# Layer 0's first product in a four-layer graph network: seven block products for eight from the fifth unit on, and group weights in two rotating buffers

## The chip, the cores and the metric

The kernel runs on one core of a Trainium2 chip. Its time is the device time of one execution in microseconds (us). Before the change the median of three runs is 2221.21 us (2220.69 to 2221.58). One more execution was profiled; it took 2220.84 us, and its span, from the first to the last instruction in the trace, is 2218.8 us.

The engines are named as in the profile: PE is TensorE (matmul), PEld its weight load, DVE is VectorE, ACT is ScalarE, POOL is GpSimd, and SP is SyncE, which here only issues DMAs. [...]

## The reference

The input is 128 graphs of 64 nodes with 256 features in float32, with one 64x64 adjacency matrix per graph. Four layers follow each other, each as `x = layernorm(x + layer(x, adj))`. The change touches layer 0. It works on five groups of nodes (25, 9, 7, 6 and 6 nodes out of the first 25), each with two graph convolutions of its own weights:

```python
A = adj + eye; dinv = deg ** -0.5; norm_adj = dinv * A * dinv
support = einsum('bnd,de->bne', x, W)          # W1: 256 x 512, then W2: 512 x 256
out = relu(einsum('bnm,bme->bne', norm_adj, support) + b)
...
h     = graph_conv(x[:, idx], adj[:, idx][:, :, idx], W1[g], b1[g])
out_g = graph_conv(h,         adj[:, idx][:, :, idx], W2[g], b2[g])
fused[:, idx] += softmax(fusion_w)[g] * out_g
```

Layers 1 and 2 are graph convolutions over all 64 nodes. Layer 3 is a gated recurrent cell, run five times per graph; it takes most of the time.

## The kernel before

Layer 0 packs graphs block-diagonally. A tile holds as many graphs as fit into 126 rows, and a unit is four tiles, up to 504 columns (UNITS, L61). The groups come in the order 1, 2, 3, 4, 0. This gives 16 units: units 0 to 2 belong to group 1 (504, 504 and 144 columns), 3 and 4 to group 2 (448 each), 5 and 6 to group 3 (504 and 264), 7 and 8 to group 4 (504 and 264), 9 to 15 to group 0 (six of 500, then 200). "The fifth unit" is unit 4.

A unit passes through these steps, each a function:

- `load0` (L342): DMAs of the adjacency blocks (`a`, L357) and of x (`xg`, L359). For groups 3 and 4 a row range is two runs of three nodes, so that a tile takes four DMAs.
- `prep` (L364): DVE adds the identity, sums the degrees (`ae`, L374), POOL raises to the power -0.5, DVE builds the block-diagonal matrix A, PE transposes it (L393), and DVE evicts and scales it to `AT` (L397).
- `aggregate` (L399): PE multiplies x by AT (`pa`, L407), ACT copies the result to `ag` (L412).
- `hidden` (L415): the first product, W1 (256 x 512) by `ag`. There are four blocks of 128 output rows by two blocks of 128 input rows: eight block products of all columns (`ph`, L422), each pair closed by a relu on ACT into `hg` (L425).
- `support` (L428): `hg` by W2, tile by tile, in two halves of two tiles (`ps`, L436).
- `add` (L449): PE multiplies by AT once more (`po`, L458), ACT scales and applies relu, DVE adds into F.
- `finish` (L484), for group 0 only: transposes back, adds the residual, layer norm, stores.

A loop (L565) runs a software pipeline over these units. Iteration i issues the loads of unit i+3, `add` of i-1, `aggregate` of i+1, `support` of i, `finish` of i-1, `prep` of i+2 and `hidden` of i+1. PE runs in exactly the order in which this is written (the manual schedule, L329). The other engines' order is made by a scheduler from priorities, from `high_priority` blocks and from `issue_after`, which pins an instruction behind another. In the same iterations `others` (L514) normalises the 39 nodes that layer 0 leaves as they are (`xo`, loaded at L511, stored at L520), and the steps of layers 1 and 2 for the first two chunks of graphs (`mid`, L219) begin.

All group weights are resident: W1 for five groups and W2 for five groups, one DMA of 512 KB each (L534, L537). Those of groups 1 and 2 are issued ahead of the loop's iteration 0, that of W1 for group 3 in iteration -1, and the other five in iteration 0.

Layer 3 computes its gates with seven block products for eight already (class `Gates`, L695): a 2x2-block product in the Strassen-Winograd form. `factors` (L660) makes the three combined weight blocks, `sums` (L687) the combined inputs on POOL, and the seven products go into three PSUM banks, a, b and d, with copies on ACT (L727) and adds on DVE (L729, L733, L739).

Of the kernel before, what the change touches and what calls it, by code (L numbers as in the profile page):

```python
# [16 lines left out]
NG, NJ = 5, 25  # L17
# [50 lines left out]
def gnn_stack(  # L68
# [118 lines left out]

    def load_adj(c):
        a64 = keep.tile([128, NP, N], F32, name="a64", bufs=2)
        nc.sync.dma_start(a64, av[c])  # L190
        adjs[c] = a64
# [140 lines left out]
    with ExitStack() as c0:  # L332
        w0 = c0.enter_context(tc.tile_pool(name="w0", bufs=1))
        work = c0.enter_context(tc.tile_pool(name="work0", bufs=1))
        W1 = w0.tile([128, NG, 2, HID], F32, name="W1")
        W2 = w0.tile([128, NG, 4, D], F32, name="W2")
# [3 lines left out]
        loads, A, AG, HG, S2, Z, XO = {}, {}, {}, {}, {}, {}, {}  # L340

# [73 lines left out]
        def hidden(i):  # L415
            u = UNITS[i]
            ag0 = AG.pop(i)
            hg = keep.tile([128, 4, 512], F32, tag="NI", name="hg", bufs=2)
            for e in range(4):
                p = psum0("ph")[:, : u.cols]  # L420
                for k in range(2):
                    nc.tensor.matmul(  # L422
                        p, W1[:, u.g, k, e * 128 : (e + 1) * 128], ag0[:, k, : u.cols], start=k == 0, stop=k == 1
                    )
                nc.scalar.activation(hg[:, e, : u.cols], p, AF.Relu, bias=b1[:, u.g * 4 + e : u.g * 4 + e + 1])  # L425
            HG[i] = hg

        def support(i):  # L428
            u = UNITS[i]
            hg, s2 = HG.pop(i), []  # L430
            for v in range(0, len(u.tiles), 2):
                p = psum0("ps").rearrange("p (t d) -> p t d", t=2)
                ts = range(v, min(v + 2, len(u.tiles)))
                for t in ts:
                    for e in range(4):
                        nc.tensor.matmul(  # L436
                            p[: u.rows[t], t - v, :], hg[:, e, u.off[t] : u.off[t] + u.rows[t]], W2[:, u.g, e, :],
                            start=e == 0, stop=e == 3,
                        )
# [93 lines left out]
        def load_first(g):  # L533
            nc.sync.dma_start(W1[:, g], w1[g].rearrange("(k p) e -> p k e", p=128))  # L534

        def load_second(g):
            nc.sync.dma_start(W2[:, g], w2[g].rearrange("(k p) e -> p k e", p=128))  # L537
# [26 lines left out]
        g0 = next(i for i, u in enumerate(UNITS) if u.g == 0)  # L564
        for i in range(-2, NU + 1):  # L565
            if i >= 0:
                stage(load0, i + 3)
            stage(add, i - 1)
            if i:
                stage(aggregate, i + 1)  # L570
            early_stage(i, 0)
            stage(support, i)
            if not i:
                aggregate(1)
            if i == NU:
# [3 lines left out]
            if i == -1:  # L579

                hidden(0)
                with tc.issue_after(evictions[0].ins):
                    prep(1)
            else:
                stage(prep, i + 2)
                stage(hidden, i + 1)
# [5 lines left out]
            elif i == -1:  # L592
                load_second(2)
                load_first(3)
            elif i == 0:
                load_second(3)
                for g in (4, 0):
                    load_first(g)
                    load_second(g)
# [60 lines left out]
    def factors(w, w21):  # L660

        nc.vector.tensor_add(w[:, 4, :], w21, w[:, 3, :])
        nc.gpsimd.tensor_sub(w[:, 6, :], w[:, 0, :], w21)
        nc.vector.tensor_sub(w[:, 5, :], w[:, 4, :], w[:, 0, :])
        nc.vector.tensor_sub(w[:, 2, :], w[:, 1, :], w[:, 5, :])
# [21 lines left out]
    def sums(a, name):  # L687

        t = work.tile([128, 4, H], F32, tag="T" + name, name="T" + name, bufs=2)
        nc.gpsimd.tensor_sub(t[:, 0:2, :], a[:, :, H:], a[:, 0, :].rearrange("p (s n) -> p s n", s=2))  # L690
        nc.gpsimd.tensor_sub(t[:, 2, :], a[:, 1, H:], t[:, 0, :])
        nc.gpsimd.tensor_sub(t[:, 3, :], a[:, 1, :H], t[:, 2, :])
        return t

    class Gates:  # L695

        def __init__(self, C, sides, name):
            self.C, self.sides, self.name = C, sides, name  # L700
            self.copies = {}

        def multiply(self, bank, i):
            for g, side in enumerate(self.sides):
                for m, (w, q, a, t) in enumerate(side):
                    rhs = {
                        1: a[:, 0, :H], 2: a[:, 1, :H], 3: a[:, 1, H:], 4: t[:, 3, :], 5: t[:, 0, :], 6: t[:, 2, :],
                        7: t[:, 1, :],
                    }[i]
                    nc.tensor.matmul(  # L710
                        bank[:, g, :], w[:, q, i - 1, :], rhs, start=i in (1, 2, 5) and g == 0 and m == 0,
                        stop=m == len(side) - 1, skip_group_check=True,
                    )

        def bank(self, s):
            return pg.tile([128, 2, H], F32, tag="pg", name=f"p{s}{self.name}")

        def product(self, i):
            C = self.C
            if i == 1:  # L720
                self.a = self.bank("a")
            if i in (1, 6, 7, 4):
                self.multiply(self.a, i)
                if i != 4:
                    c = self.copies[i] = work.tile([128, 2, H], F32, tag="copy", name=f"c{i}", bufs=4)
                    with tc.high_priority():
                        nc.scalar.copy(c, self.a)  # L727
                if i == 7:
# [245 lines left out]
```

## Time and profile before

| | before |
|---|---|
| runs, median (lowest to highest) | 2221.21 us (2220.69 to 2221.58) |
| span of the profiled execution | 2218.8 us |
| mean granted PE clock | 0.993 |
| PE busy | 2180.1 us, 98% |
| DVE / ACT / POOL busy | 1376.3 / 1004.5 / 582.5 us |
| layer 0's stretch | from 0 to about 308 us |
| `hidden`, a unit of 500 columns | 6.71 us on the chain |

The page gives busy time by engine, then 40 slices of the span with one digit each (tenths busy), and the clock that PE was granted. A group of instructions has its line of the kernel, its engine, what it writes and reads, its count, busy time and mean duration. In a timeline, a bracket at the end of a line gives the idle time of the engine ahead of it and what released it. A windows row gives, for a stretch of the span, the busy time of PE, PEld, DVE, ACT and POOL (with instruction counts), the clock, the share of the DMA engines and their GB/s.

### The profile page before, as it was taken

The numbers are of one execution on the slowest core, as the hardware profiler recorded it, in microseconds if no ns is written. First come the engines' busy times: TensorE is split into PE (matmuls) and PEld (weight loads), VectorE is DVE, ScalarE is ACT, GpSimd is POOL, SyncE is SP. The second block draws the span as 40 slices with busy tenths as digits, with TensorE's granted clock in tenths as the row PEclk, the third lists the DMA queues.
The fourth block names the chain that finished last, engine by engine and source line by source line (L and its number), as shares of the span: only waits on it lengthen the run. The fifth ranks groups of instructions, "written<-read, shape, count | busy, mean of one in ns | idle before, by whom it ended". The sixth has DMA issues, their size and how long they took to land.

```text
span 2218.8 us, 30141 instructions
## 1 busy us (share of the span) xinstructions
PE 2180.1 (98%) x11526; PEld 1912.2 (86%) x11526; DVE 1376.3 (62%) x3068; ACT 1004.5 (45%) x1850; POOL 582.5 (26%) x639
## 2 busy tenths in 40 slices
PE   7999999999999999999999999999999999999997
PEld 5677888888888889888889898888898898888886
DVE  4443667666766666666756676657666666556546
ACT  2333334445544454445454454455454544455443
POOL 3210123222222223223222222222222222222222
PEclk9999999999999999999999999999999999999998
DMA  6540210000100000000100010001000000000000
GB/s 188 169 128 22 57 46 3 1 3 1 40 2 3 1 20 22 4 1 8 34 1 3 1 41 1 4 1 41 1 1 1 20 10 1 1 10 10 1 1 20
DMA packets 54172, 51.12 MB, mean 23 GB/s; under 512 B 20878, under 2 KB 49036, under 8 KB 54028
## 3 DMA queue, kind: packets, MB, share of 16 engines
q1 hardware_dynamic: 49524, 43.90, 6.5%
q0 software_dynamic: 1936, 4.83, 0.7%
q8 instruction: 91, 1.49, 0.3%
q10 hardware_dynamic: 2568, 0.47, 0.1%
q14 instruction: 53, 0.43, 0.1%
HBM read 32.40 MB, written 16.78 MB: 22 GB/s over the span
## 4 chain that ended last, share of the span: by engine, by line
PE 91%; DMA 3%; DVE 2%; issue 1%; SPq 1%; POOL 1%; ACT 0%; POOLq 0%; ACTq 0%; DVEq 0%
PE parz L710 25%; PE pdrz L710 12%; PE pan L710 12%; PE pa L209 9%; PE pbrz L710 6%; PE pdn L710 6%; PE pT L751 4%; PE pbn L710 3%; PE ph L422 3%; PE ps L436 3%; PE pd L285 2%; PE pd L306 2%; DMA xo<-in_x_dram 1%; PE pa L407 1%; PE po L458 1%
## 5 line engine op out<-in xcount | busy, mean ns | idle before, releaser
L727 ACT COPY c<-parz 128x512 f32<-128x512 f32 x240 | 140.9, 587 | 322.5 <-PE parz L710 322.0
L710 PE MATMUL parz<-Th,WHH 128*128 128x256 f32 x960 | 285.8, 379 | 0.0
L710 PE MATMUL parz<-Ta,V 128*128 128x256 f32 x960 | 285.5, 379 | 0.0
L690 POOL TENSOR_TENSOR Th<-hn 128x512 f32<-128x512 f32 x64 | 81.6, 1274 | 774.0 <-DVE hn L811 588.5
L808 ACT ACTIVATE NI<-NI,bih 128x512 f32<-128x512 f32 x160 | 115.6, 722 | 206.2 <-DVE NI L804 206.1
L727 ACT COPY c<-pan 128x512 f32<-128x512 f32 x240 | 141.0, 587 | 149.6 <-PE pan L710 149.6
L710 PEld LDWEIGHTS parz<-Ta,V 128*128 128x128 f32 x960 | 182.4, 190 | 24.7
L710 PEld LDWEIGHTS parz<-Th,WHH 128*128 128x128 f32 x960 | 176.2, 190 | 20.9 <-ACT c L727 0.2
L781 ACT ACTIVATE RZ<-RZ,brz 128x512 f32<-128x512 f32 x160 | 116.1, 727 | 138.6 <-DVE RZ L739 138.6
L690 POOL TENSOR_TENSOR Ta<-agg 128x512 f32<-128x512 f32 x80 | 102.2, 1277 | 260.6 <-ACT agg L213 260.6
L739 DVE TENSOR_TENSOR RZ<-pdrz,c 128x512 f32<-128x512 f32 x80 | 55.1, 688 | 173.9 <-PE pdrz L710 173.9
L710 PE MATMUL pan<-Ta,V 128*128 128x256 f32 x480 | 143.2, 380 | 0.9 <-ACT c L727 0.9
L710 PE MATMUL pan<-Th,WHH 128*128 128x256 f32 x480 | 142.7, 379 | 0.0
L138 POOL TENSOR_TENSOR rs<-ve,mhalf 128x4 f32<-128x4 f32 (+2 forms) x66 | 68.7, 1042 | 252.3 <-DVE ve L136 226.4
L733 DVE TENSOR_TENSOR NI<-pbn,c 128x512 f32<-128x512 f32 x80 | 55.4, 692 | 127.6 <-PE pbn L710 108.6
L209 PEld LDWEIGHTS pa<-A,h 128*128 128x128 f32 x1024 | 124.4, 192 | 3.3
L729 DVE TENSOR_TENSOR NI<-pdn,c 128x512 f32<-128x512 f32 x80 | 55.2, 690 | 114.4 <-ACT c L727 114.4
L209 PE MATMUL pa<-A,h 128*128 128x128 f32 x1024 | 124.6, 275 | 0.0
L809 DVE TENSOR_TENSOR RZ<-hn,NI 128x512 f32<-128x512 f32 x128 | 87.9, 687 | 48.5 <-ACT NI L808 48.5
L811 DVE TENSOR_TENSOR hn<-RZ,NI 128x512 f32<-128x512 f32 x160 | 109.9, 687 | 1.8
L810 DVE TENSOR_TENSOR RZ<-RZ 128x512 f32<-128x512 f32 x160 | 109.7, 685 | 1.8
L436 PE MATMUL ps<-W,hg 128*125 128x256 f32 (+5 forms) x464 | 104.2, 382 | 0.0
(199 smaller groups left out, 5076.1 us busy)
## 6 DMA issues: line engine op xcount, KB each, us to landing
out_dram<-xt SPq DMA_DIRECT2D x32, 256.0 KB
W<-in_w_dram SPq DMA_DIRECT2D x10, 512.0 KB
xt<-xb SPq DMA_DIRECT2D x32, 156.0 KB
xo<-in_x_dram SPq DMA_DIRECT2D x9, 512.0 KB
xb<-xo SPq DMA_DIRECT2D x9, 512.0 KB
xt<-xa SPq DMA_DIRECT2D x32, 100.0 KB
xg<-in_x_dram SPq DMA_DIRECT2D x25, 125.0 KB
xa<-xg SPq DMA_DIRECT2D x25, 125.0 KB
```

The lines of the kernel that those rows point to most:

```text
L138: nc.gpsimd.tensor_tensor(rs[:r, :n], ve[:r, :n], mhalf[:r, :n], ALU.pow)
L209: nc.tensor.matmul(p[:, q * 128 : (q + 1) * 128], src[:, q, k * 128 : (k + 1) * 128], m[:, q, :], start=True, stop=True)
L436: nc.tensor.matmul(p[: u.rows[t], t - v, :], hg[:, e, u.off[t] : u.off[t] + u.rows[t]], W2[:, u.g, e, :], start=e == 0, stop=e == 3,)
L690: nc.gpsimd.tensor_sub(t[:, 0:2, :], a[:, :, H:], a[:, 0, :].rearrange("p (s n) -> p s n", s=2))
L710: nc.tensor.matmul(bank[:, g, :], w[:, q, i - 1, :], rhs, start=i in (1, 2, 5) and g == 0 and m == 0, stop=m == len(side) - 1, skip_group_ ...
L727: nc.scalar.copy(c, self.a)
L751: nc.tensor.transpose(p[:, q * 128 : (q + 1) * 128], src(q, k), ident)
L781: nc.scalar.activation(RZ[:, q, 0, :], RZ[:, q, 0, :], AF.Sigmoid, bias=b[0])
L808: nc.scalar.activation(n, n, AF.Tanh, bias=bih[:, 4 + j : 5 + j])
L809: nc.vector.tensor_sub(d, self.hT[:, j, :], n)
L810: nc.vector.tensor_mul(d, d, z)
L811: nc.vector.tensor_add(self.hn[:, j, :], d, n)
```

## The change

- `hidden` becomes a generator. For units 4 to 14 it forms the first product by seven block products of half the columns each, two output halves per product: 14 matmuls of half width for 8 of full width. Units 0 to 3 and unit 15 (200 columns, less than H = 256) keep eight.
- Its products are spread over PE's order: the generator is advanced twice ahead of the second half of `support` of the unit before (it sets up the sums, then runs product 1), three times after `prep` (products 6, 2, 5), once more at the end (7), once after the next `add` (4), and to its end after the next `aggregate` (3).
- `factors`, `sums` and `Gates` move up, so that both layers use them; for layer 0, three copies of bank a on ACT and three adds on DVE join the products, and eight relus of half width stand for four.
- The weights of a group live in two rotating buffers. W1 is loaded by four DMAs (three into a tile with room for seven blocks, one into a separate tile W21), W2 by one. Groups 3, 4 and 0 are loaded in iterations 2 and 3, 4 and 5, 6 and 7. The combined weight blocks are made in iterations 1, 3, 5 and 7, pinned behind the latest AT eviction and power.

```diff
+    def factors(w, w21):
+
+        nc.vector.tensor_add(w[..., 4, :], w21, w[..., 3, :])
+        nc.gpsimd.tensor_sub(w[..., 6, :], w[..., 0, :], w21)
+        nc.vector.tensor_sub(w[..., 5, :], w[..., 4, :], w[..., 0, :])
+        nc.vector.tensor_sub(w[..., 2, :], w[..., 1, :], w[..., 5, :])
+
...
+    def sums(a, pool, name, bufs=2):
+
+        h = a.shape[2] // 2
+        t = pool.tile([128, 4, H], F32, tag="T" + name, name="T" + name, bufs=bufs)[:, :, :h]
+        nc.gpsimd.tensor_sub(t[:, 0:2, :], a[:, :, h:], a[:, 0, :].rearrange("p (s n) -> p s n", s=2))
+        nc.gpsimd.tensor_sub(t[:, 2, :], a[:, 1, h:], t[:, 0, :])
+        nc.gpsimd.tensor_sub(t[:, 3, :], a[:, 1, :h], t[:, 2, :])
+        return t
...
+        def product(self, i):
+            C, h = self.C, self.h
+            if i == 1:
+                self.a = self.bank("a")
+            if i in (1, 6, 7, 4):
+                self.multiply(self.a, i)
+                if i != 4:
+                    c = self.pool.tile([128, 2, H], F32, tag="copy", name=f"c{i}", bufs=4)[:, :, :h]
+                    self.copies[i] = c
+                    with tc.high_priority():
+                        nc.scalar.copy(c, self.a)
+                if i == 7:
+                    nc.vector.tensor_add(C[:, :, 1, h:], self.d, self.copies.pop(7))
+            elif i == 2:
+                b = self.bank("b")
+                self.multiply(b, i)
+                nc.vector.tensor_add(C[:, :, 0, :h], b, self.copies.pop(1))
+            else:
+                if i == 5:
+                    self.d = self.bank("d")
+                self.multiply(self.d, i)
+                if i == 3:
+                    nc.vector.tensor_add(C[:, :, 0, h:], self.d, self.copies.pop(6))
...
-        W1 = w0.tile([128, NG, 2, HID], F32, name="W1")
-        W2 = w0.tile([128, NG, 4, D], F32, name="W2")
...
+        W1, W21, W2 = {}, {}, {}
...
-        def hidden(i):
+        def hidden(i, seven=True):
+
             u = UNITS[i]
-            ag0 = AG.pop(i)
+            w, w21 = W1[u.g], W21[u.g]
+            ag0 = AG.pop(i)[:, :, : u.cols]
             hg = keep.tile([128, 4, 512], F32, tag="NI", name="hg", bufs=2)
-            for e in range(4):
-                p = psum0("ph")[:, : u.cols]
-                for k in range(2):
-                    nc.tensor.matmul(
-                        p, W1[:, u.g, k, e * 128 : (e + 1) * 128], ag0[:, k, : u.cols], start=k == 0, stop=k == 1
-                    )
-                nc.scalar.activation(hg[:, e, : u.cols], p, AF.Relu, bias=b1[:, u.g * 4 + e : u.g * 4 + e + 1])
             HG[i] = hg
+            b = lambda e: b1[:, u.g * 4 + e : u.g * 4 + e + 1]
+            if not seven or u.cols < H:
+                for _ in range(5):
+                    yield
+                for e in range(4):
+                    p = psum0("ph")[:, : u.cols]
+                    for k in range(2):
+                        wk = w21[:, e // 2, :] if e % 2 > k else w[:, e // 2, 3 if e % 2 else k, :]
+                        nc.tensor.matmul(p, wk, ag0[:, k, :], start=k == 0, stop=k == 1)
+                    nc.scalar.activation(hg[:, e, : u.cols], p, AF.Relu, bias=b(e))
+                return
+            h = u.cols // 2
+            with tc.high_priority():
+                t = sums(ag0, work, "0", 1)
+            C = hg.rearrange("p (g j) n -> p g j n", g=2)[:, :, :, : u.cols]
+            g7 = Gates(C, [[(w, g, ag0, t)] for g in range(2)], work, lambda s: psum0("ph" + s))
+            for m in (1, 6, 2, 5, 7, 4, 3):
+                yield
+                g7.product(m)
+                for g in range(2):
+                    j, f = {2: (0, slice(0, h)), 7: (1, slice(h, 2 * h)), 3: (0, slice(h, 2 * h))}.get(m, (1, slice(0, h)))
+                    if m in (2, 7, 3, 4):
+                        nc.scalar.activation(C[:, g, j, f], C[:, g, j, f] if m != 4 else g7.a[:, g, :], AF.Relu, bias=b(2 * g + j))
 
         def support(i):
+
             u = UNITS[i]
             hg, s2 = HG.pop(i), []
             for v in range(0, len(u.tiles), 2):
+                yield v + 2 >= len(u.tiles)
                 p = psum0("ps").rearrange("p (t d) -> p t d", t=2)
                 ts = range(v, min(v + 2, len(u.tiles)))
                 for t in ts:
                     for e in range(4):
                         nc.tensor.matmul(
-                            p[: u.rows[t], t - v, :], hg[:, e, u.off[t] : u.off[t] + u.rows[t]], W2[:, u.g, e, :],
+                            p[: u.rows[t], t - v, :], hg[:, e, u.off[t] : u.off[t] + u.rows[t]], W2[u.g][:, e, :],
                             start=e == 0, stop=e == 3,
                         )
...
         def load_first(g):
-            nc.sync.dma_start(W1[:, g], w1[g].rearrange("(k p) e -> p k e", p=128))
+            W1[g] = w0.tile([128, 2, 7, 128], F32, tag="W1", name=f"W1{g}", bufs=2)
+            W21[g] = w0.tile([128, 2, 128], F32, tag="W21", name=f"W21{g}", bufs=2)
+            v = w1[g].rearrange("(k p) (q e) -> p k q e", p=128, q=2)
+            for k in range(2):
+                nc.sync.dma_start(W1[g][:, :, k, :], v[:, k, :, :128])
+            nc.sync.dma_start(W21[g], v[:, 0, :, 128:])
+            nc.sync.dma_start(W1[g][:, :, 3, :], v[:, 1, :, 128:])
 
         def load_second(g):
-            nc.sync.dma_start(W2[:, g], w2[g].rearrange("(k p) e -> p k e", p=128))
+            W2[g] = w0.tile([128, 4, D], F32, tag="W2", name=f"W2{g}", bufs=2)
+            nc.sync.dma_start(W2[g], w2[g].rearrange("(k p) e -> p k e", p=128))
...
+        cur = iter(())
         for i in range(-2, NU + 1):
             if i >= 0:
                 stage(load0, i + 3)
             stage(add, i - 1)
+            next(cur, None)
             if i:
                 stage(aggregate, i + 1)
+            for _ in cur:
+                pass
             early_stage(i, 0)
-            stage(support, i)
+
+            nxt = hidden(i + 1, i > 2) if 0 <= i + 1 < NU else iter(())
+            if 0 <= i < NU:
+                for last in support(i):
+                    if last and i:
+                        next(nxt, None)
+                        next(nxt, None)
+            else:
+                next(nxt, None)
+                next(nxt, None)
             if not i:
                 aggregate(1)
+                next(nxt)
+                next(nxt)
             if i == NU:
                 folds = [products(0, q) for q in range(3)]
             stage(finish, i - 1, g0)
             early_stage(i, 1)
             if i == -1:
 
-                hidden(0)
+                for _ in nxt:
+                    pass
                 with tc.issue_after(evictions[0].ins):
                     prep(1)
             else:
                 stage(prep, i + 2)
-                stage(hidden, i + 1)
+                for _ in range(3):
+                    next(nxt, None)
+            next(nxt, None)
+            cur = nxt
             if i == -2:
                 load0(1, powers[0])
                 load_second(1)
...
                 load_first(2)
             elif i == -1:
                 load_second(2)
-                load_first(3)
-            elif i == 0:
-                load_second(3)
-                for g in (4, 0):
-                    load_first(g)
-                    load_second(g)
+
+            elif i == 1:
+                with tc.issue_after(evictions[-1].ins), tc.issue_after(powers[-1].ins):
+                    factors(W1[2], W21[2])
+            elif i in (2, 4, 6):
+                g = {2: 3, 4: 4, 6: 0}[i]
+                load_first(g)
+            elif i in (3, 5, 7):
+                g = {3: 3, 5: 4, 7: 0}[i]
+                load_second(g)
+                with tc.issue_after(evictions[-1].ins), tc.issue_after(powers[-1].ins):
+                    factors(W1[g], W21[g])
...
-    def sums(a, name):
-
-        t = work.tile([128, 4, H], F32, tag="T" + name, name="T" + name, bufs=2)
-        nc.gpsimd.tensor_sub(t[:, 0:2, :], a[:, :, H:], a[:, 0, :].rearrange("p (s n) -> p s n", s=2))
-        nc.gpsimd.tensor_sub(t[:, 2, :], a[:, 1, H:], t[:, 0, :])
-        nc.gpsimd.tensor_sub(t[:, 3, :], a[:, 1, :H], t[:, 2, :])
-        return t
```

In layer 3 only the arguments change (`sums(..., work, ...)`, `Gates(..., work, lambda s: bank(...))`).

More of the change, by code (lines that the diff above doesn't have):

```diff
@@ new lines, in gnn_stack, with __init__, multiply, bank @@
+    class Gates:
+        def __init__(self, C, sides, pool, bank):
+            self.C, self.sides, self.pool, self.new_bank = C, sides, pool, bank
+            self.h = C.shape[3] // 2
+            self.copies = {}
+        def multiply(self, bank, i):
+            h = self.h
+            for g, side in enumerate(self.sides):
+                for m, (w, q, a, t) in enumerate(side):
+                    rhs = {
+                        1: a[:, 0, :h], 2: a[:, 1, :h], 3: a[:, 1, h:], 4: t[:, 3, :], 5: t[:, 0, :], 6: t[:, 2, :],
+                        7: t[:, 1, :],
+                    }[i]
+                    nc.tensor.matmul(
+                        bank[:, g, :], w[:, q, i - 1, :], rhs, start=i in (1, 2, 5) and g == 0 and m == 0,
+                        stop=m == len(side) - 1, skip_group_check=True,
+                    )
+        def bank(self, s):
+            return self.new_bank(s)[:, : 2 * self.h].rearrange("p (g n) -> p g n", g=2)
+        def product(self, i):
[21 more added lines that the diff above has]
+                    nc.vector.tensor_add(C[:, :, 0, h:], self.d, self.copies.pop(6))
@@ L658, in gnn_stack @@
     V = [work.tile([128, 3, 7, 128], F32, name=f"V{l}") for l in range(L)]
[L660 to L665, printed above, removed]
     def fold():
@@ L685, in fold, with bank @@
                 yield
-    def sums(a, name):
-        t = work.tile([128, 4, H], F32, tag="T" + name, name="T" + name, bufs=2)
-        nc.gpsimd.tensor_sub(t[:, 0:2, :], a[:, :, H:], a[:, 0, :].rearrange("p (s n) -> p s n", s=2))
-        nc.gpsimd.tensor_sub(t[:, 2, :], a[:, 1, H:], t[:, 0, :])
-        nc.gpsimd.tensor_sub(t[:, 3, :], a[:, 1, :H], t[:, 2, :])
-        return t
[L695 to L728, printed above, removed]
-                    nc.vector.tensor_add(C[:, :, 1, H:], self.d, self.copies.pop(7))
-            elif i == 2:
-                b = self.bank("b")
-                self.multiply(b, i)
-                nc.vector.tensor_add(C[:, :, 0, :H], b, self.copies.pop(1))
-            else:
-                if i == 5:
-                    self.d = self.bank("d")
-                self.multiply(self.d, i)
-                if i == 3:
-                    nc.vector.tensor_add(C[:, :, 0, H:], self.d, self.copies.pop(6))
+    def bank(s):
+        return pg.tile([128, 2 * H], F32, tag="pg", name="p" + s)
     class Chunk:
@@ L759, in state_of_layer2 @@
             if not k:
-                self.th = sums(self.hT, "h")
+                self.th = sums(self.hT, work, "h")
         def messages(self, h=None):
             self.agg = gather(self.xt if h is None else h, self.A01, "agg", work, "agg", 2)
-            self.ta = sums(self.agg, "a")
+            self.ta = sums(self.agg, work, "a")
         def rz(self, i):
@@ L769, in rz @@
                 self.g = Gates(
-                    self.RZ, [[(WHH, q, self.hT, self.th), (V[self.l], q, self.agg, self.ta)] for q in (0, 1)], "rz"
+                    self.RZ, [[(WHH, q, self.hT, self.th), (V[self.l], q, self.agg, self.ta)] for q in (0, 1)],
+                    work, lambda s: bank(s + "rz"),
                 )
@@ L786, in n @@
                 self.gn = Gates(
-                    self.NI, [[(V[self.l], 2, self.agg, self.ta)], [(WHH, 2, self.hT, self.th)]], "n"
+                    self.NI, [[(V[self.l], 2, self.agg, self.ta)], [(WHH, 2, self.hT, self.th)]],
+                    work, lambda s: bank(s + "n"),
                 )
@@ L826, in turn @@
                 if not k:
-                    self.th = sums(self.hT, "h")
+                    self.th = sums(self.hT, work, "h")
             else:
```

## The prediction

> **What bounds the kernel now.** I read the page first: the shares, the slices with the clock, the chain by engine.
>
> ```profile
> span 2218.8 us, 30141 instructions
> PE 2180.1 (98%) x11526; PEld 1912.2 (86%) x11526; DVE 1376.3 (62%) x3068; ACT 1004.5 (45%) x1850; POOL 582.5 (26%) x639
> PE   7999999999999999999999999999999999999997
> PEclk9999999999999999999999999999999999999998
> ```
>
> TensorE is busy 98% of the span at full clock. A micro-second of its work saved is a micro-second of time, unless a wait fills it. Layer 0 ends near 308 us, so I then read the chain of work up to 335 us, for what one matmul record costs (each F32 matmul leaves two records):
>
> ```profile
> 161.19 1.78 PE po L458 x16
> 157.62 3.56 PE ph L422 x16
> 181.08 6.91 PE ps L436 x32
> 188.42 6.71 PE ph L422 x16
> ```
>
> hidden() (ph) takes 6.71 us for 16 records of 500 columns: 419 ns each. support (ps) takes 6.91 / 32 = 216 ns at 256 columns; po takes 1.78 / 16 = 111 ns at 126. So a record costs 0.833 ns per column plus about 3 ns. The weight load of about 190 ns that each carries doesn't show, even at 126 columns.
>
> Third, the timeline of TensorE around its gaps, and the windows of 25 us (length; busy PE, PEld, DVE, ACT, POOL with counts; clock; DMA share; GB/s):
>
> ```profile
> 93.47 3.59 PE L407 MATMUL pa<-AT,xg 126*128 126x126 f32 x16 [2.60 <-DVE AT L397]
> 112.85 1.90 PE L407 MATMUL pa<-AT,xg 126*128 126x126 f32 x12
> 130.04 3.07 PE L407 MATMUL pa<-AT,xg 126*128 126x126 f32 x16 [2.41 <-DVE AT L397]
> ...
> 75.00:100.00 25.00, 22.40 (x106) 17.42 (x105) 11.15 (x55) 7.32 (x12) 10.76 (x14) 0.93 0.64 198
> 225.00:250.00 25.00, 25.00 (x137) 20.03 (x137) 15.92 (x48) 8.01 (x13) 3.41 (x3) 1.00 0.27 77
> ```
>
> TensorE waits for AT of units 5 and 7 for 2.60 and 2.41 us, and the work behind takes 3.59 and 3.07 us instead of 1.90: 1.7 and 1.2 us more, at a granted clock of 0.93. With 0.65 us at 73.70 this stage loses 8.5 us. From 133 us on it loses nothing until 328 us.
>
> What holds AT back is in the timelines of SP and VectorE:
>
> ```profile
> 28.45 0.59 SPq L537 DMA_DIRECT2D W<-in_w_dram  x1
> 29.09 0.51 SPq L534 DMA_DIRECT2D W<-in_w_dram  x1
> 29.64 0.47 SPq L537 DMA_DIRECT2D W<-in_w_dram  x1
> 30.15 0.51 SPq L534 DMA_DIRECT2D W<-in_w_dram  x1
> 30.70 0.47 SPq L537 DMA_DIRECT2D W<-in_w_dram  x1
> ...
> 86.78 0.74 SPq L359
> 90.38 0.26 DVE L374 TENSOR_TENSOR ae<-a,eye 126x12 f32<-126x12 f32 x2 [4.55 <-DMA xb<-xo]
> 92.74 0.68 DVE L397 TENSOR_TENSOR AT<-pT,d0o 126x504 f32<-126x504 f32 x1
> ```
>
> SP issues the small loads of groups 3 and 4 at 0.79 us each, one after another, from 50 to 131 us. VectorE runs in order and waits for them (4.55 us at 90.38), and the AT multiply stands behind. So up to 133 us the queue SP, then DVE, then PE sets the time; after that TensorE alone.
>
> **What the Trainium skill says.** "TensorE: Matmul & The Clock Gate", section "Back-to-back issue gap": start to start is N/2.4 + 2.5 ns warm. Two passes per record fit my 0.833 ns per column. "Part 1: The HAM clock gate" halves the rate after at least one idle window of about 3.4 us and restores it after about 3.4 us of work; here gaps of 2.60 and 2.41 us were enough to slow what followed, so I count shorter gaps as dangerous too. "Perfetto Trace Analysis", section "Tensor Engine Instruction", calls ACT and DVE strictly first in, first out; the 90.38 line shows it. "DMA: Bandwidth & Descriptors", "Specifications", asks 512 B for line rate: the new pieces of W1 have just 512 B rows; no run here shows what they cost.
>
> **The change, part by part.**
>
> Removed and added on TensorE: 16 records of all columns become 28 of half. At 500: 28 x 211 = 5.91 against 6.71, saves 0.80. At 504 also 0.80; at 448, 28 x 189.4 = 5.30 against 16 x 376 = 6.01, saves 0.71; at 264, 28 x 113 = 3.16 against 3.56, saves 0.40. Units 4 to 14: 0.71 + 2 x 0.80 + 2 x 0.40 + 6 x 0.80 = 7.9 us, of which 3.1 in units 4 to 8 and 4.8 in 9 to 14. The loops of layers 1 to 3 keep their order, so what is saved ahead of them stays saved.
>
> Added elsewhere, per 500-column unit, by rows of layer 3, which has the same helpers:
>
> - POOL: three subtractions, priced by the row of 1277 ns and that of 728 twice: 2.7 us. Before, POOL is busy 3.4 in 25.
> - ACT: three copies at 587 (row L727) and eight half-width relus for four whole. A relu of 264 columns takes 482, of 500 takes 677: 1.76 + 8 x 0.48 - 4 x 0.68 = +2.9 us, onto 8.0 in 25.
> - DVE: three adds at 0.69: 2.1 us, onto 15.9 in 25.
>
> From unit 9 on all of this lies beside TensorE's 24 us. What shows is latency: product 4 goes into bank a and must wait for ACT's copy of product 7. Between them stands add, 1.78 us; the copy takes 0.59, and two relus of 0.48 may stand before it. Bounds 0 and 0.5 us per unit; I take 0.1. The second half of support needs product 3, its DVE add 0.69 and relu 0.48; 8 records of ps, 1.7 us, cover that when DVE is not late.
>
> Factors of four groups: three DVE and one POOL operation of 256 columns each, some 0.4 and 0.75 us: 1.3 us of DVE per group, in iterations 1, 3, 5, 7. Free by time, but they stand in DVE's order.
>
> Moved: each group's load is five DMAs for two, 15 more issues at about 0.5 us; but those of groups 3, 4 and 0 leave 28 to 31 us and go behind units 5 to 10. SP loses 2.8 us of issues there and most of some 7 us for which unit 4's loads crawled behind those 2.5 MB (16 loads from 32.3 to 48.8 us; at unit 5's pace 12). By unit 5 SP is some 7 to 10 us early; it gives back about 2.5 us at each later group. Queued behind them on SP are xo and the loads of the next units, for which the layer norms and ae on DVE wait. New there too: a load into a rotating buffer waits for TensorE's last read of the group before; SP stands meanwhile. Bounds: 0 (read long done) to 3 us (SP had that lead); inside the lead I take 0.
>
> New waits in units 4 to 8: product 4 of unit 4 needs the copy of product 7, on ACT behind the relus of product 2, which need a DVE add; that add stands behind AT of unit 5 (92.74 before, some 1.5 us earlier now). Add 0.69, relus 1.0, copy 0.5 with hand-overs: about 95.7. TensorE is there at 90: a gap of 5 to 6 us where before were 2.60 and 1.7 of slow clock. So unit 4 costs 1 to 3 us before its saving; I take 2.0. With 0.8 + 0.4 saved in units 5 and 6 TensorE comes to the aggregate of unit 7 about when it does now. AT of unit 7 I take 0.9 us earlier (DVE's added operations eat most of SP's lead), and a gap of 1.5 us as too short to slow the clock (2.05 us of work after the 0.65 at 73.70): 0.9 + 1.2 = 2.1 us back, with bounds of 0 and 3.6. Support of unit 6 and product 4 of units 7 and 8 wait for DVE adds behind a64 loads and block operations: 0 to 3 us together, I take 1.5, against 1.2 saved in 7 and 8.
>
> Sum: unit 4, +2.0 less 0.7; units 5 and 6, -1.2; the gap at 130, -2.1; units 7 and 8, +1.5 - 1.2; units 9 to 14, -4.8 + 0.6; the change of layers, where 2.17 us are idle at 328, +0.7. That is -5.2 us: span 2213.6. Runs stand 2.0 above the profiled span (2220.84 for 2218.8), and the median at 2221.21: 2216.0.
>
> **Rivals.**
>
> - Full gain. SP's lead shortens both old gaps and no new one opens: 7.9 plus 1.5 to 4 of the 8.5 us: 2211 (2207 to 2213.5). For it: the windows give DVE 15 of 25 busy, so there is room. Against: AT waits for order, not for room.
> - No change. Units 4 to 8 lose the 4.2 that 9 to 14 give: 2220 (2218 to 2223). For it: to 133 us TensorE isn't the bound.
> - Slower. VectorE's order: the adds of products 2, 7 and 3 are queued behind DVE operations that wait for loads, and TensorE can't pass product 4, 3 or support. Five units at 2.5 to 3 us, each gap with 1.2 to 1.7 of slow clock, make 15 us or more against 7.9: 2226 (2223 to 2232). It decides from 8 us of such gaps on. For it: the 4.55 at 90.38. Against: after 133 us DVE has idle stretches up to 7.75 us ahead of AT.
> - That seven products are not run at all is excluded by TensorE's order, where product 4 of a unit stands between po and pa.
>
> **How the numbers follow.** The likeliest 0.45 (own range 2213 to 2219), full gain 0.20, no change 0.17, slower 0.18. A 0.2% step is 4.44 us, about what a measurement here tells from nothing: the bound is 2216.8. Two thirds of the likeliest and all of the full gain lie below it: 0.50. A third of the likeliest and nearly all of no change: 0.32. Slower: 0.18. The range of 2210 to 2225.5 leaves out a third of the full gain and two thirds of the slower case.
>
> **What would show it.** PE records of half width at 211 ns where ph stood; chain steps of 5.9 for 6.7 us per unit, and no gap, in 150 to 300 us. One gap at product 4 of unit 4 with DVE or ACT as releaser, near 96 us, and no more 2.41 at the aggregate of unit 7. POOL rows 40 up. The prediction is wrong if PE gaps at product 4 or support appear in several units after 133 us, if SP waits for TensorE before a group's load, or if product 4 waits in every unit from 9 on.

## The result and the profile after

The changed kernel takes 2229.43 us (median of four runs, 2229.04 to 2232.06) against 2220.95 us before: 8.5 us slower, ratio 1.0040 with a 95% interval of 1.0025 to 1.0055. The forecast was 2216.0 us. The number of the third rival, "slower" (2223 to 2232 us), came true.

The page of the changed kernel, the lines that answer to those of before:

```profile
span 2227.3 us, 30602 instructions
PE 2175.1 (98%) x11658; PEld 1935.6 (87%) x11658; DVE 1402.7 (63%) x3113; ACT 1026.8 (46%) x1927; POOL 611.3 (27%) x676
PE   7899989999999999999999999999999999999997
PEclk9899999999999999999999999999999999999998
```

TensorE is busy 5.0 us less and the span is 8.5 us longer: about 13.5 us more are idle. The timeline of TensorE names them. These are its gaps from unit 3 on, with the idle time and what ended it in the bracket:

```profile
60.63 3.76 PE L473 MATMUL pa<-AT,xg 112*128 112x112 f32 x16 [6.81 <-DVE AT L463]
97.43 1.83 PE L221 MATMUL pha<-T,W 128*128 128x224 f32 x4 [6.00 <-ACT c L239]
139.81 2.75 PE L522 MATMUL ps<-W,hg 128*126 128x256 f32 x8 [3.11 <-ACT hg L510]
240.38 1.16 PE L544 MATMUL po<-AT,s 125*128 125x125 f32 x8 [0.23 <-DVE xt L356]
241.82 1.16 PE L544 MATMUL po<-AT,s 125*128 125x125 f32 x8 [0.28 <-DVE xt L356]
281.06 1.16 PE L275 MATMUL pa<-AT,xt 128*128 128x128 f32 x8 [0.82 <-DVE poly L336]
291.39 1.16 PE L544 MATMUL po<-AT,s 125*128 125x125 f32 x8 [0.34 <-DVE xt L356]
336.86 1.12 PE L810 MATMUL pT<-ident,xt 128*128 128x128 f32 x4 [7.75 <-ACT hT L817]
```

They are the aggregate of unit 3, product 4 of unit 4, the second tile of support of unit 6, some small ones beside layers 1 and 2, and the first work of layer 3. Before, that last gap was 2.17 us at 328.22.

The start times of the same matmuls in both traces show where the time went. "Weights alone" is the second experiment below.

| TensorE starts (us) | before | after | weights alone |
|---|---|---|---|
| aggregate of unit 3 | 59.70 | 60.63 | 63.06 |
| of unit 5 | 93.47 | 99.06 | 95.98 |
| of unit 7 | 130.04 | 132.58 | 130.25 |
| of unit 9 | 162.81 | 167.39 | 163.10 |
| of unit 12 | 215.69 | 217.49 | 215.99 |
| of unit 15 | 290.96 | 293.24 | 291.25 |
| second transpose of layer 3 | 328.22 | 336.86 | 331.92 |
| span | 2218.8 | 2227.3 | 2222.4 |

In the after column, product 3 of the unit before an aggregate still follows that aggregate (0.45 us for a short unit, 0.85 for a long one). With this the delay is 3.1 us at unit 15, and the change of layers adds 5.5. From there to the end nothing more is lost. So the question has two parts: what costs 5.5 us at the change of layers, and why 7.9 us less arithmetic left layer 0 3.1 us later.

For the first part, POOL's timeline. Before:

```profile
324.32 0.80 POOL L670 DMA_DIRECT2D wh<-in_whhT_dram  x1
```

After:

```profile
331.87 0.80 POOL L780 DMA_DIRECT2D wh<-in_whhT_dram  x1 [4.46 <-DMA xa<-xg]
335.48 0.67 ACT L791 COPY w<-pf 128x128 f32<-128x128 f32 x2 [6.39 <-POOL V L191]
```

POOL now stands 4.46 us at the load of `wh`, a small weight tile of layer 3, until stores of x (`xa<-xg`) have landed. Behind it on POOL are the operations that form layer 3's weights; ACT's copies wait for these (6.39 us), and TensorE for ACT. The cause is placement. `wh` lies at bytes 172480 to 174016 of a partition in both programs. Before, the x tiles of units 11 and 12 lay there, long stored. Layer 0's weight pool is now 16 KB smaller, so that the tiles above it slid down, and the x tiles of units 13 and 14 lie there. Those are among the last that layer 0 stores.

For the second part, VectorE ahead of the gap at 97.43:

```profile
89.33 0.75 DVE L133 BATCH_NORM_STATS2 st<-xo 128x6 f32<-128x256 f32 x2 [3.88 <-DMA xo<-in_x_dram]
...
92.41 1.38 DVE L153 TENSOR_SCALAR xo<-xo,mv,rs 128x256 f32<-128x256 f32 x4 [1.12 <-POOL rs L138]
93.71 0.68 DVE L463 TENSOR_TENSOR AT<-pT,d0o 126x504 f32<-126x504 f32 x1
...
95.37 0.62 DVE L245 TENSOR_TENSOR hg<-phb,c 128x448 f32<-128x448 f32 x1
```

The add of product 2 (`hg<-phb,c`) stands behind AT, and AT behind a layer norm that waited 3.88 us for its rows. TensorE had produced product 2 at 88. Before the gap at 139.81 the order is again at fault, though less for a wait than for a full queue: product 3 is done at 135, and its add is issued 4 us later. Ahead of it stands `Ab`, an operation of layers 1 and 2 that waited 1.36 us for its adjacency load, then adds into F and more of layers 1 and 2; VectorE is busy all that time:

```profile
134.62 0.69 DVE L291 TENSOR_TENSOR Ab<-a,pair 128x512 f32<-128x512 f32 x1 [1.36 <-DMA a<-in_adj_dram]
...
138.91 0.42 DVE L251 TENSOR_TENSOR hg<-phd,c 128x264 f32<-128x264 f32 x1
```

### The profile page after: what moved, and what is told of

It is laid out like the page before. It is cut to its first block, busy times and chain, and to the rows that moved or that the text cites. A ratio compares the mean times of both kernels' runs of the same rounds, so it can differ in the third digit from the quotient of the medians.

```text
span 2227.3 us, 30602 instructions
## 1 busy us (share of the span) xinstructions
PE 2175.1 (98%) x11658; PEld 1935.6 (87%) x11658; DVE 1402.7 (63%) x3113; ACT 1026.8 (46%) x1927; POOL 611.3 (27%) x676
## 4 chain that ended last, share of the span: by engine, by line
PE 90%; DVE 3%; DMA 2%; issue 2%; POOL 1%; SPq 1%; ACT 0%; POOLq 0%; ACTq 0%; DVEq 0%
PE parz L221 25%; PE pdrz L221 12%; PE pan L221 12%; PE pa L275 9%; PE pbrz L221 6%; PE pdn L221 6%; PE pT L810 4%; PE ps L522 3%; PE pbn L221 3%; PE pd L372 2%; PE pd L351 2%; PE pha L221 1%; PE pa L473 1%; DMA xo<-in_x_dram 1%; PE pf L639 1%
```

## The experiments

Each group of runs had the kernel before beside it on the same chip. Its median there was 2221.23 us in the first group, 2220.37 in the second, 2221.43 in the third, 2220.94 in the last. I compare by the ratio; the times of two groups can be up to 1 us apart for this alone.

**1. The place of wh.**

```diff
+    w21h = work.tile([128, 3, 128], F32, name="wh21")
     WHH = work.tile([128, 3, 7, 128], F32, name="WHH")
...
-        w21 = work.tile([128, 3, 128], F32, name="wh21")
+        w21 = w21h
```

> After, with one edit: the small weight tile of layer 3 (wh) is allocated first in its pool, so that it lies where F lay and not where the x tiles of units 13 and 14 lay. Theory A (the change of layers costs 5.6 us more than before, because wh now stands on x tiles whose stores to memory must land first): PE's gap of 7.75 us at 336.86 shrinks to about 2, and the time falls by 5 to 6 us, to 2223.5 to 2224.5. Rival B (the gap comes from DVE and ACT being later by the added adds, copies and relus): under 1 us of change, 2228.5 to 2229.5.

Measured: 2225.69 us, ratio 1.0019 (1.0010 to 1.0028): 3.7 us under the changed kernel. The gap:

```profile
332.70 1.12 PE L811 MATMUL pT<-ident,xt 128*128 128x128 f32 x4 [3.22 <-ACT hT L818]
```

7.75 has become 3.22 us, and POOL issues the load of `wh` without a wait. The mechanism holds; the size is smaller than expected, since 1.0 us of the gap comes from elsewhere (run 10; run 9 agrees).

**2. The weights alone.**

```diff
-            nxt = hidden(i + 1, i > 2) if 0 <= i + 1 < NU else iter(())
+            nxt = hidden(i + 1, False) if 0 <= i + 1 < NU else iter(())
...
-                    factors(W1[g], W21[g])
```

> The weights part alone: rotating buffers, five DMAs per group, late loads, but eight block products for every unit (no sums, copies or factors in layer 0). Theory A (the change of layers, +5.6, and the gap ahead of the aggregate of unit 3 come from the weights' part; the start is 6 us earlier too): slower than before in spite of unchanged arithmetic, 2225 to 2228, with the gap of 6.8 at about 60 and the one of some 7.8 at about 337. Rival C (all of the loss comes from the seven products' chains through DVE and ACT): 2215 to 2221, as before or better.

Measured: 2223.83 us, ratio 1.0013 (1.0006 to 1.0020), span 2222.4. This is slower than before, as theory A says, but 1.2 us under its range. The table above shows that from unit 7 to unit 15 this kernel stands within 0.3 us of before, and that it loses 3.4 us at the change of layers:

```profile
331.92 1.12 PE L805 MATMUL pT<-ident,xt 128*128 128x128 f32 x4 [5.57 <-ACT w L786]
```

It also has the gap ahead of unit 3 (6.18 us at 63.06). That gap eats up an earlier start and more: hidden of unit 0 begins at 16.2 us where it began at 19.46, since the load that ACT's first activation waits for lands at 14.09 and not at 17.35, and unit 3's aggregate still comes 3.4 us later than before. By unit 7 the two are level, since of the old waits for AT, 2.60 and 2.41 us, only 0.65 (unit 5) and 1.21 (unit 6) are left.

**3. Seven products only for units 9 to 14.**

```diff
-            nxt = hidden(i + 1, i > 2) if 0 <= i + 1 < NU else iter(())
+            nxt = hidden(i + 1, i > 7) if 0 <= i + 1 < NU else iter(())
...
+                    if g == 0:
                         factors(W1[g], W21[g])
```

> Seven products for units 9 to 14 only, factors for group 0 only, all else as after. If each of the six units gives its 0.80 us and nothing waits there: 4.8 us less than the kernel with eight products everywhere, so 2220 to 2223 under theory A. If product 4 or the second half of support wait in each of these units (0.5 us or more each), less than 2 us less. Against after: the gap of 6.0 at product 4 of unit 4 and that of 3.1 at support of unit 6 are gone; if those cost what they show, this is 3 to 6 us faster than after (it gives back 3.1 us of arithmetic).

Measured: 2235.88 us, ratio 1.0070 (1.0055 to 1.0085). A clear miss: slower than with eleven units. The gaps of 6.00 and 3.11 are gone (4.43 at 61.14 and 2.28 at 114.10 are left early on), but TensorE has new ones:

```profile
213.89 2.04 PE L544 MATMUL po<-AT,s 125*128 125x125 f32 x8 [3.88 <-DVE AT L327]
216.80 2.07 PE L544 MATMUL po<-AT,s 125*128 125x125 f32 x8 [0.86 <-ACT z L548]
...
267.84 3.48 PE L372 MATMUL pd<-L2W,ag 128*128 128x256 f32 x8 [2.71 <-ACT v L378]
...
272.48 1.16 PE L544 MATMUL po<-AT,s 125*128 125x125 f32 x8 [1.16 <-ACT v L378]
274.50 2.07 PE L544 MATMUL po<-AT,s 125*128 125x125 f32 x8 [0.86 <-ACT z L548]
```

The `po` matmul reads nothing that L327 writes. What they share is a PSUM bank: in this program both `po` tiles of unit 10 lie in bank 6 (the expectation of run 6 calls it unit 11), in which the transposed adjacency of the first chunk (`pT1`) waits for VectorE. In the changed kernel they lie in banks 4 and 2. The gaps from 267 on are of the same kind: both `po` tiles of unit 12 lie in bank 5, with the two `pd` tiles that ACT reads (`v`). Layer 0 takes its tiles in turn from two pools, five and three in eight; a unit with seven products takes three tiles for four. So the choice of units shifts every later tile. Run 6 tests this.

**4. The layer norms behind AT.**

```diff
+                        pin = EV.get(i + 1) if f is others else None
+                        with tc.issue_after(pin) if pin is not None else nullcontext():
                             f(o)
```

`EV` holds each unit's AT eviction.

> After, with each layer norm of the 39 other nodes pinned behind the AT eviction of the next unit in DVE's order (no wait, order alone). Theory D (the gaps at 60.6 and 97.4 come from AT and the product adds standing behind layer norms that wait for their DMAs): both gaps fall below 2 us and the time falls by 4 to 8 us, to 2221.5 to 2225.5. Rival E (the loads on SP set the pace up to 130 us whatever the order on DVE): the gaps move to later aggregates, under 2 us of change, 2227.5 to 2229.5.

Measured: 2230.79 us, ratio 1.0046 (1.0031 to 1.0061). The gap at 60 fell from 6.81 to 2.03, that at 97 to 4.20, now behind POOL, and one of 8.59 opened at product 4 of unit 6:

```profile
87.25 1.86 PE L221 MATMUL pha<-T,W 128*128 128x224 f32 x4 [4.20 <-POOL T L200]
134.20 1.22 PE L221 MATMUL pha<-T,W 128*128 128x132 f32 x4 [8.59 <-ACT c L239]
```

VectorE's timeline says why: the scheduler moved `Ab` of layers 1 and 2 to the front, and VectorE waits 14.91 us for its load, with AT and the product adds behind it.

```profile
131.39 0.69 DVE L291 TENSOR_TENSOR Ab<-a,pair 128x512 f32<-128x512 f32 x1 [14.91 <-DMA a<-in_adj_dram]
```

Neither theory's number came: by the intervals this is no different from the changed kernel (1.0025 to 1.0055). The gaps moved, as rival E has it, but to a place that VectorE's order makes and not SP's pace.

**5. The weights alone, wh first.** Runs 1 and 2 together.

> The weights part alone (eight products everywhere, as in the run before it) with wh allocated first. Theory A (what the weights part costs is only the place of wh in memory, 3.6 us at the change of layers): within 1 us of the kernel before, 2220.2 to 2222.2, and PE's gap at about 330 back to 2 to 3 us. Rival (later loads, more DMAs or DVE's order cost time too): 2223 to 2225, as without the move.

Measured: 2220.81 us, ratio 1.0001 (0.9993 to 1.0010), the same as before. TensorE's gap is back at its old size:

```profile
328.92 0.66 PE L806 MATMUL pT<-ident,xt 128*128 128x128 f32 x4 [2.15 <-ACT w L787]
```

From the aggregate of unit 15 to this transpose it is 37.26 us, to the hundredth what it was before. So rotating buffers, twenty smaller loads and later loading cost nothing by themselves; what the weights part costs is where `wh` came to lie.

**6. Seven late, wh first, the PSUM tiles shifted.**

```diff
             h = u.cols // 2
+            if i == 9:
+                for _ in range(3):
+                    psum0("skip")
```

> Seven products for units 9 to 14 only, wh first, and three PSUM tiles taken and not used ahead of unit 9, so that the PSUM tiles rotate from there on as in the changed kernel. Theory F (the gaps of 3.88, 0.86, 2.71, 1.16 and 0.86 between 213 and 275 in the run with seven late come from the rotation: both po tiles of unit 11 fell into the bank that held the transposed adjacency of the first chunk until DVE had evicted it): these gaps vanish, and the time is 2216.5 to 2220, that is 2 to 4.8 us under the kernel before. Rival G (DVE is too full in this stretch with the product adds, whatever the bank): gaps of 2 us and more remain there, 2226 or more.

Measured: 2220.20 us, ratio 1.0001 (0.9993 to 1.0010). The large gaps of run 3 between 213 and 275 are gone; the largest left there is 0.28 us. Theory F stands on that; the edit also moved `wh`, which lies outside this stretch. The gain is under the forecast (2216.5 to 2220): unit 15's aggregate comes at 288.66 and in run 5 at 291.66, 3.0 us earlier, or 2.1 with product 3 counted. At the change of layers the rest goes.

**7. wh first, the first operations of layers 1 and 2 behind AT.** The pin of run 4, but around `next(early)` in place of the layer norms.

> After with wh first and the first operations of layers 1 and 2 (Ab and so on, which wait for a64 loads) pinned on DVE behind the AT eviction of the unit of the next iteration. Theory D2 (support of unit 6 waits 3.1 us and then runs at the slow clock because the add of product 3 stands behind Ab on DVE): against the run with wh first alone (2225.7) 3 to 5 us less, 2220.5 to 2222.5. Rival E (loads set the pace): the gap moves to the next unit, within 1.5 us of 2225.7.

Measured: 2223.01 us, ratio 1.0013 (1.0004 to 1.0021). That is 2.7 us under run 1 and just outside theory D2's range; by the ratios it is 1.3 us, and the intervals overlap, so the time alone doesn't decide between D2 and E. The traces do: the gap at support of unit 6 fell from 3.66 to 0.97 us, no gap took its place in the next units, and unit 14's aggregate starts at 259.81 where it was 267.00 in run 1. Another opened at 277.18 (3.72 us, ended by `poly`, L336). The pin also held back the second chunk, and I took that for the cause.

**8. Both pins.**

> As the run before it, with the layer norms of the 39 other nodes pinned behind the next unit's AT too. Theory D (DVE's order makes all the gaps of units 3 to 8): no gap over 2.5 us between 80 and 160, 2216 to 2220. Rival E (loads set the pace there, and stores of normalised rows that come later hold up SP): a gap of 3 us or more at another place before 160, 2222 or more.

Measured: 2218.46 us, ratio 0.9989 (0.9982 to 0.9997), slightly faster than before and in theory D's range; between 80 and 160 no gap is over 2.10 us, as it has it. Unit 14's aggregate starts at 256.98 where it was 264.96. Then the gap of run 7 comes again:

```profile
132.52 1.99 PE L523 MATMUL ps<-W,hg 128*126 128x256 f32 x8 [1.41 <-ACT hg L511]
274.34 2.08 PE L275 MATMUL pa<-AT,xt 128*128 128x128 f32 x8 [3.72 <-DVE poly L336]
```

**9. wh first, PSUM tiles shifted ahead of unit 15** (three tiles skipped, as in run 6).

> After with wh first and three PSUM tiles taken and not used ahead of unit 15, so that the tiles rotate through the change of layers as in the kernel before (eleven units take three tiles for four: 11 fewer, which is 3 fewer than a whole turn of 8). Theory F: the 1.8 us that the change of layers still takes more than before (39.1 against 37.3 from unit 15's aggregate to the second transpose) are gone; against the run with wh first (2225.7, span 2224.1) about 2 us less, a span of 2221.5 to 2222.5. Rival (DVE or POOL set that stretch): no change of it.

Measured: 2224.89 us, ratio 1.0015 (1.0008 to 1.0022), against 1.0019 for run 1: 0.8 us less where 2 were expected, with overlapping intervals. No trace of this run is used. Alone, it decides nothing.

**10. All repairs**: wh first, layer norms pinned, only the first operations of the first chunk pinned, three tiles skipped ahead of unit 15.

> After with all repairs: wh first, layer norms of the other nodes and the first operations of layers 1 and 2 of the first chunk alone pinned behind AT on DVE, and three PSUM tiles skipped ahead of unit 15. If the 7.9 us of arithmetic were lost to DVE's order, to the place of wh and to the rotation, and to nothing else: unit 14's aggregate near 257 (before 265), no gap of 3.72 at 274, and 2211 to 2214.5. Rival (DVE is too full around 225 to 330 for seven products with layers 1 and 2 beside them): 2216 or more, with DVE as the releaser of gaps after 225.

Measured: 2216.67 us, ratio 0.9979 (0.9970 to 0.9989). This is 4.8 us under the kernel before and so faster than both, but not the 2211 to 2214.5 expected. The rival's number, 2216 or more, came without its mechanism: the gaps that VectorE ends after 225 us are the small ones of the changed kernel, 1.65 us in all, and the one of 3.72 is 0.80. TensorE's larger gaps, and POOL ahead of the first:

```profile
84.09 1.02 POOL L122 TENSOR_TENSOR d0r<-d0s,mhalf 126x4 f32<-126x4 f32 x1 [7.20 <-DVE d0s L120]
...
85.79 1.86 PE L221 MATMUL pha<-T,W 128*128 128x224 f32 x4 [5.80 <-POOL T L200]
129.94 1.99 PE L526 MATMUL ps<-W,hg 128*126 128x256 f32 x8 [1.41 <-ACT hg L514]
197.06 5.41 PE L526 MATMUL ps<-W,hg 128*125 128x256 f32 x16 [2.13 <-ACT hg L514]
...
323.86 0.70 PE L819 MATMUL pT<-ident,xt 128*128 128x128 f32 x4 [2.15 <-ACT w L800]
```

At 323.86 the gap is the 2.15 us of before, where runs 1, 6, 7 and 8 had 3.2 us ended by `hT`: from unit 15's aggregate 38.09 us, in run 8 39.08. So the shift is worth 1.0 us there (run 10 differs from run 8 in one pin too, but run 9 adds the shift alone and is 0.8 us less), and 0.85 of what remains over 37.26 is product 3. At 85.79 POOL's sums stand behind a power (`d0r`), which waits for VectorE and through it for a load. The gap of 2.13 at 197 costs almost twice its length, for the 16 records behind it take 5.41 us where the same 16 take 3.62 at full clock.

**11. The kernel before with the pins of run 10.**

> The kernel before with the same two pins (layer norms and first operations of layers 1 and 2 behind AT on DVE) and nothing else. If DVE's order alone made the gaps of 2.60 and 2.41 and the slow clock behind them: 3 to 8 us less, 2213 to 2218, and the repairs would be worth as much without seven products. If SP's loads set the pace of groups 3 and 4 before: within 2 us of before, 2219 to 2223.

Measured: 2218.32 us, ratio 0.9987 (0.9981 to 0.9994). About 3 us of run 10's gain are to be had without seven products. The time lies between the two forecasts, and the trace gives each a half: the gap of 2.41 ahead of unit 7 is gone, so that one was made by VectorE's order; the one ahead of unit 5 grew from 2.60 to 5.98, behind an `ae` for which VectorE stood 11.90 us until a DMA had landed:

```profile
95.27 3.75 PE L408 MATMUL pa<-AT,xg 126*128 126x126 f32 x16 [5.98 <-DVE AT L397]
```

**12. Run 10, POOL's powers behind the sums of the unit before.**

```diff
+                with tc.issue_after(LS[0]) if LS[0] is not None else nullcontext():
                     stage(prep, i + 2)
```

`LS[0]` is the last subtraction of the sums.

> As the run with all repairs, with one more pin: on POOL the power of a unit's degrees stands behind the sums of the unit before it. There product 4 of unit 4 waited 5.80 us for POOL's sums, which stood behind a power whose input waited for a load. If that order makes the gap: it falls under 2 us, and the time by 3 to 6 us against that run (2216.7), to 2211 to 2214. If the loads of that unit set the pace (the next AT needs the same power): the gap moves to the next aggregate, 2215 to 2218.

Measured: 2216.17 us, ratio 0.9980 (0.9973 to 0.9987), no different from run 10. That is the number of the second forecast, but not its mechanism. Unit 7's aggregate starts at 116.82 us, 13 us ahead of the kernel before, and then it is lost again:

```profile
84.53 0.99 PE L223 MATMUL pha<-T,W 128*128 128x224 f32 x4 [2.29 <-ACT c L241]
123.44 3.13 PE L528 MATMUL ps<-W,hg 128*126 128x256 f32 x8 [2.49 <-ACT hg L516]
157.51 3.06 PE L528 MATMUL ps<-W,hg 128*126 128x256 f32 x8 [2.32 <-ACT hg L516]
...
271.59 2.08 PE L277 MATMUL pa<-AT,xt 128*128 128x128 f32 x8 [3.69 <-DVE poly L338]
```

The gap of 5.80 has become 2.29, and the adds of product 3 fall behind other work on VectorE at units 6 and 8. The gap of 3.69 is that of runs 7 and 8, although only the first chunk is pinned here; so the pin of the second chunk isn't its only cause. With each edit the scheduler orders VectorE anew.

## Why the prediction was wrong

The steps of its sum, each with what the traces show for the same stretch, product 3 counted where it belongs:

| step | predicted | measured |
|---|---|---|
| to the end of unit 7's aggregate (unit 4, units 5 and 6, the gap at 130) | -2.0 | +1.9 |
| from there to unit 9 (units 7 and 8) | +0.3 | +3.1 |
| units 9 to 14 | -4.2 | -1.9 |
| change of layers | +0.7 | +5.5 |
| sum | -5.2 | +8.6 |

**The change of layers is the step that failed worst.** I gave it 0.7 us without looking at what the smaller weight pool would do to the tiles that come after it. Runs 1, 2 and 5 show the place of `wh` as the cause: from unit 15's aggregate to the second transpose run 1 takes 39.09 us where the changed kernel takes 43.62, so 4.5 of the 5.5 us. Run 10 puts the other 1.0 down to the PSUM rotation. What failed is the assumption that a smaller pool and fewer PSUM tiles move nothing but the work they serve.

**The arithmetic was right.** The chain of the changed kernel has four records of 250 columns in 0.84 us, 210 ns each against 211 predicted:

```profile
178.24 0.84 PE phd L221 x4
179.08 0.84 PE pha L221 x4
179.93 1.72 PE po L544 x12
```

**Unit 4: right mechanism, wrong size.** A gap of 5 to 6 us at product 4, near 96, with ACT or DVE as releaser: it is 6.00 at 97.43, ended by ACT's copy. I left the slow clock behind it out: product 4 takes 1.83 us where its neighbours take 0.92, and the aggregate 3.62 for 1.90. That is 2.6 us more. The way to the gap was off too: AT of unit 5 comes at 93.71, not 1.5 us ahead of 92.74, and two of the new factors (`W`, L190 and L192, 0.42 us each) stand between it and the add. "Perfetto Trace Analysis", section "Tensor Engine Instruction", of the Trainium skill calls ACT and DVE strictly first in, first out; this trace agrees, with a product add issued 7 us after its product, behind a layer norm's wait of 3.88.

**Unit 3: no term.** The gap of 6.81 us ahead of its aggregate and the slow clock behind it (3.76 for 1.94) stand nowhere in the sum. They eat up an earlier start (hidden of unit 1 at 32.47 for 38.52), and support of unit 3 begins 2.7 us late (64.18 for 61.48). VectorE's order sets the end of the next gap, at product 4 of unit 4, so this delay probably adds nothing behind it; no run shows that alone.

**The gap at 130: right in sign, wrong in its reason.** The gap and the slow clock behind it are gone, 3.6 us where I took 2.1. But AT came only 0.6 us earlier (128.74 for 129.31); TensorE came later, 6.8 us behind at support of unit 4 (103.67 for 96.89) and 1.9 behind at that of unit 6. The old gap took up most of the new delay, and nothing was gained.

**SP's lead: about right in size, without the effect.** Loads of unit 5 begin at 38.45 us in place of 49.52, 11 us early for the 7 to 10 that I took. In the new order on VectorE a layer norm and the `ae` of unit 5, which wait for loads (1.79 and 3.41 us), stand ahead of AT of unit 3, which comes at 59.96 us where it came at 57.93. The wait of 4.55 us at 90.38, which the prediction puts down to the loads alone, is ended in the profile by a store of normalised rows (`xb<-xo`); the last load for that unit was issued 4.4 us earlier, at 85.99, so either may have come last.

**Units 7 and 8: too small.** I took 1.5 us for waits; against this stand 4.3 us (3.1 and the 1.2 saved), of which one gap of 3.11 with the slow clock behind it makes up most.

**Units 9 to 14: half right.** Between the aggregates of units 9 and 12 the time fell by 2.8 us (50.10 for 52.88); 0.4 of it is product 3, which at the later mark is the longer one, and 2.4 are three times 0.80, as the arithmetic says. From 12 to 15 it rose by 0.5 (75.75 for 75.27): there layers 1 and 2 share VectorE, and the 1.67 us of small gaps with DVE as releaser lie there. The bound "0 to 0.5 us per unit" was put on the copy for product 4; the waits come by PSUM tiles instead. The `po` tiles of unit 11, which wait at 240.38 and 241.82, lie in banks 7 and 6, with the `pd` tiles of layer 1 that VectorE still reads (`xt`, L356).

The rival "slower" named VectorE's order as its mechanism. That is what cost most in layer 0, with gaps of 6.81, 6.00 and 3.11 us and not five of 2.5 to 3. It didn't name memory placement, from which 5.5 of the 8.6 us come; that its number came true is in part luck. "No change" fell: what 9 to 14 gave didn't balance units 4 to 8.

Open: whether the full 7.9 us can be had. Run 10 collects 4.8 us, and run 11 gets 3 of them without the seven products; their intervals (0.9970 to 0.9989 and 0.9981 to 0.9994) overlap. Whether VectorE has room for all of it, or only lacks the right order, is open too: every pin mended one gap, and another opened elsewhere. Seven products with the weights of all five groups resident and loaded early weren't tried.

## What to carry to other kernels

A cheaper product with a chain of copies, adds and relus between its parts gave its arithmetic here only where those engines' queues held nothing that waited for a load: read what stands ahead of each added operation in its engine's order. When a pool shrinks or a tile is taken less often, list what the next stage's tiles come to lie on and who releases it, in SBUF and in the rotation of PSUM; here the two cost 5.5 us at the change of layers, where the arithmetic saves 7.9. Undo the accidental part first: one allocation moved gave back 3.7 us.

## What was unexpected of the hardware

The length of a gap alone doesn't decide whether the clock drops. In run 5 the clock fell to half behind a gap of 1.80 us, and the twelve records of unit 6's aggregate took 2.91 us where they take 1.9 at full clock:

```profile
114.61 2.91 PE L473 MATMUL pa<-AT,xg 126*128 126x126 f32 x12 [1.80 <-DVE AT L463]
```

In run 12 it stayed full behind a longer gap, the 2.29 us at 84.53 shown above. What decides is where a gap falls. In the clock that the traces record, the stretches at half clock, but for the one at the end of each, last 3.41 us (24 of them), 6.83 (21) or 10.24 (5), so one, two or three times 3.41. I laid windows of 3.41 us on these steps in the thirteen traces with a clock record, up to 2150 us, and added up TensorE's idle time in each window at full clock:

| idle in a window of 3.41 us | windows | followed by half clock |
|---|---|---|
| under 1.6 us | 7979 | 0 |
| 1.6 to 2.0 us | 13 | 8 |
| 2.0 us and more | 42 | 42 |

So it takes about half a window. The 1.80 us of run 5 lie within one window, from 111.81 to 115.22 us; the 2.29 us of run 12 fall into two, 0.94 and 1.35. In run 6 the clock fell too, behind a gap of 2.77 us ahead of the same aggregate:

```profile
115.02 2.10 PE L473 MATMUL pa<-AT,xg 126*128 126x126 f32 x12 [2.77 <-DVE AT L463]
```

Its twelve records are hardly slower only because the window ended late, at 116.74, when most of them were done; the support behind them paid. Every 3.41 us at half clock cost up to 1.7 us of TensorE's work (half of 3.41). This is read from the traces; no run was made to test it.

"TensorE: Matmul & The Clock Gate", "Part 1: The HAM clock gate", of the Trainium skill calls the windows free-running and about 3.4 us long, and the steps agree with both. It asks for at least one idle window before the clock halves. A drop after 1.80 us of idle time doesn't fit that, and the measurement decides.
